# Residual product of an attention layer taken into the seven-product accumulation

## The chip, the cores and the metric

The kernel runs on one core of a Trainium2 chip. The metric is the device time in microseconds (us) of one execution. An engine runs its own instructions in the order in which the program gives them: PE (matrix products), DVE (vector), ACT (scalar functions), POOL and SP. SP and ACT also issue the DMA transfers here, in line with their other instructions.

## The reference, cut to what matters

Two layers work on x of shape (2, 512, 64, 64). Layer 0 (a deformable convolution) is not touched by the change. Layer 1 is attention over the 4096 pixels of each image, after a group normalization:

```
px = _gn(x) as (pixels, 512)
q, k = tanh(px @ Wq.T), tanh(px @ Wk.T)          # 64 features
scores = einsum('bip,bjp,p->bij', q, k, align_w)
content = px + softmax(scores) @ (px @ Wv.T)
content = content @ Wfc.T + bfc
out = relu(batch_norm(content)); x = x + out
```

The kernel takes Wfc into the values: content @ Wfc.T is px @ Wfc.T (the residual product) plus softmax(scores) @ (px @ (Wv.T @ Wfc.T)).

## The kernel before

Layer 1 handles one image after the other. First it projects keys and queries (`pk`, L1233) and values (`values`, L1196 to L1213: product `pv`, blocks stored to DRAM as `v_d`), in four rounds `i` of two pixel chunks each. Then it goes over eight query chunks `qb` of 512 pixels. For a chunk, the 4096 keys are taken as NPAIR = 16 pairs of two key blocks of 128.

`produce(qb, kp)` (L1167) makes the scores of a pair (`pS`), their exponentials `e` as four blocks (two key blocks by two halves of 256 queries), three combinations `tt` and one `t3` of these blocks, and adds the exponentials to `tots[qb]`. It runs two pairs ahead. A pair's product with its values, a 2 by 2 block product, is done with seven block products in place of eight (Strassen's scheme in Winograd's form): `v` holds seven combinations of value blocks, `operands` gives the moving side. Six of the products are summed over the pairs in six PSUM banks, `acc[0]` to `acc[5]` (L1271), each as two products of 256 columns. The other two banks, tag `st`, hold the scores. The seventh product is summed afterwards in bank 0, as `p7` (L1322), with `v7` (128 KB, six buffers, loaded by SP) and the sixteen `t3` that were kept.

Between the pairs and `p7` the banks are put together to `ct` (L1284 to L1291): ACT copies bank 0, DVE adds the others. The sum over keys comes from `pr` = ones x `tots` in bank 1 (L1293), `rin` is its reciprocal, and `ct` is multiplied by it (L1296). `residual(cb)` (L1305) makes the residual product for 128 output channels with four products of 512 columns (`pf`, banks 1 and 2), adds it and the bias to `ct`, and takes statistics for two of the four channel blocks. `residual(0)` stands ahead of `p7`, the three others are strewn into it. `produce` for the next chunk's first two pairs stands in `p7` too. `finish_chunk` then adds `p7`, scaled by `rin`, and takes the other statistics; it is advanced during the next chunk's pairs. The pixels `xq` of a chunk are loaded at pair 2 and normalized at pair 6; `xq` and `wc` (the weights of the values) share a tag with two buffers.

The order is written out by hand (`tc.manual_schedule()`), and every engine's order is the order of emission. In the last chunk of image 0, ACT issues six chunk loads for image 1 (`chunk`, L1126). In the last chunk of image 1, the pool of the key side is closed (`inner.close()`), eight tiles `res` (`xr`, 1 MB each) are taken from its space, and ACT issues their loads (L1303). After the last `p7`, the batch statistics are put together, and sixteen chunks are scaled, added to x and stored; image 0's chunks are fetched back for that (L1372, 2 MB each).

Of the kernel before, what the change touches and what calls it, by code (L numbers as in the profile page):

```python
# [570 lines left out]
def window_path(ctx: ExitStack, tc: tile.TileContext, t_in: dict, out: bass.AP, far: bass.AP, sums: bass.AP):  # L571
# [12 lines left out]
    def load(name, shape, src=None, pool=const):  # L584
        t = pool.tile(shape, F32, name=f"{name}_sb")
        nc.sync.dma_start(t, t_in[name] if src is None else src)
        return t

    def load_w(name, cols, pool):
        return load(name, [P, KB, cols], t_in[name].rearrange("(kb p) m -> p kb m", p=P), pool)  # L590
# [497 lines left out]
    with ExitStack() as l1, tc.manual_schedule():  # L1088
# [8 lines left out]
        with ExitStack() as at, ExitStack() as inner:  # L1097
# [31 lines left out]
            def value_output():  # L1129
                t = wk.tile([P, KB, C], F32, tag="x", name="wc")  # L1130
                nc.sync.dma_start(t, wc_d)
                return t
# [15 lines left out]
            wfc = load_w("wfcT", C, aw)  # L1148
# [45 lines left out]
            def operands(e, tt):  # L1194
                return (e[:, 0, :], e[:, 2, :], tt[:, 0, :], tt[:, 1, :], e[:, 3, :], tt[:, 2, :])

            def values(i, x1, x2, t):

                cols = slice(t * P, (t + 1) * P)
                pv = []  # L1200
                for h, x in enumerate((x1, x2)):
                    p = bank(2 * (t % 2) + h, "pv")
                    for kb in range(KB):
                        nc.tensor.matmul(p, x[:, kb, cols], wc[:, kb, :], start=(kb == 0), stop=(kb == KB - 1))  # L1204
                    pv.append(p)
                v = vw.tile([P, 7, HC], F32, name="v", bufs=4)
                nc.scalar.copy(v[:, 0, :], pv[0][:, :HC])
                nc.vector.tensor_sub(v[:, 6, :], v[:, 0, :], pv[0][:, HC:])
                nc.scalar.copy(v[:, 1:6:4, :], pv[1].rearrange("p (a c) -> p a c", a=2))
                nc.vector.tensor_add(v[:, 3, :], v[:, 5, :], pv[0][:, HC:])  # L1210
                nc.vector.tensor_sub(v[:, 2, :], v[:, 3, :], v[:, 0, :])
                nc.vector.tensor_sub(v[:, 4, :], v[:, 1, :], v[:, 2, :])
                nc.sync.dma_start(v_d[n][4 * i + t], v)  # L1213

# [10 lines left out]
            for n in range(NB):  # L1225
                sc, bi = norms[n]
                ready = []
                for i in range(NCH // 2):
                    for h in range(2):
                        ch = 2 * i + h  # L1230
                        pk = bank(4 + h, "pk")
                        for kb in range(KB):
                            nc.tensor.matmul(  # L1233
                                pk, wkq[:, h, kb].rearrange("p h d -> p (h d)"), xs[ch][:, kb, :],
                                start=(kb == 0), stop=(kb == KB - 1),
                            )
                        nc.scalar.activation(kq[:, ch, :], pk, AF.Tanh)
                    if i == 0:
                        queries(0)
                    for t in range(4):  # L1240
                        values(i, xs[2 * i], xs[2 * i + 1], t)
                        if t in (0, 1) and i + 1 < NCH // 2:
                            normalize(xs[2 * i + 2 + t], sc, bi)
                        if i + 1 == NCH // 2 and t in (1, 2):
                            produce(0, t - 1)
                        if i + 1 == NCH // 2 and t > 1:
                            ready.append(load_values(n, t - 2))
# [3 lines left out]
                for qb in range(NCH):  # L1251
                    acc = {}
                    for kp in range(NPAIR):
                        if kp + 2 < NPAIR:
                            produce(qb, kp + 2)
                        nxt = qb * NPAIR + kp + 2
                        if nxt < NCH * NPAIR:
                            ready.append(load_values(n, nxt % NPAIR))
                        if kp == 2:
                            xq = wk.tile([P, KB, CH], F32, tag="x", name="xq")  # L1260
                            nc.sync.dma_start(xq, x1_d[n][qb])
                        if kp >= NPAIR - 6:
                            v7s[kp - NPAIR + 6] = load_seventh(n, kp - NPAIR + 6)
                        v = ready.pop(0)
                        e, tt, _ = made[qb, kp]
                        ops = operands(e, tt)
                        for j in (3, 4, 5, 2, 1, 0) if kp == 0 else range(6):
                            if kp == 0:
                                acc[j] = bank(j, f"acc{j}")
                            for cb in range(2):  # L1270
                                nc.tensor.matmul(  # L1271
                                    acc[j][:, cb * HQ : (cb + 1) * HQ], v[:, j, cb * P : (cb + 1) * P], ops[j],
                                    start=(kp + cb == 0), stop=(kp + cb == NPAIR),
# [11 lines left out]
                    u = [wk.tile([P, 2, HQ], F32, name=f"u{j}", bufs=1) for j in range(2)]  # L1285
                    nc.scalar.copy(u[0], a[0])
                    nc.vector.tensor_add(ct[:, 0:2, 0:HQ], u[0], a[1])
                    nc.vector.tensor_add(u[1], u[0], a[2])
                    nc.vector.tensor_add(ct[:, 2:4, HQ:], u[1], a[3])
                    nc.vector.tensor_add(ct[:, 0:2, HQ:], ct[:, 2:4, HQ:], a[4])  # L1290
                    nc.vector.tensor_sub(ct[:, 2:4, 0:HQ], u[1], a[5])  # L1291
                    pr = bank(1, "pr")
                    nc.tensor.matmul(pr, ones, tots.pop(qb), start=True, stop=True)  # L1293
                    rin = wk.tile([P, CH], F32, name="rin", bufs=1)
                    nc.vector.reciprocal(rin, pr)
# [9 lines left out]
                    def residual(cb, ct=ct, xq=xq):  # L1305
                        pf = bank(1 + (cb + 1) % 2, "pf")
                        for kb in range(KB):
                            nc.tensor.matmul(  # L1308
                                pf, wfc[:, kb, cb * P : (cb + 1) * P], xq[:, kb, :], start=(kb == 0), stop=(kb == KB - 1)
                            )  # L1310
                        nc.vector.scalar_tensor_tensor(
                            ct[:, cb, :], pf, bfc[:, cb : cb + 1], ct[:, cb, :], ALU.add, ALU.add
                        )
                        if cb < 2:
                            nc.vector.bn_stats(bst[:, cb, n * NCH + qb, :], ct[:, cb, :])

                    residual(0)
                    p7 = bank(0, "p7")
                    for kp in range(NPAIR):
                        v7, t3 = v7s.pop(kp), made.pop((qb, kp))[2]  # L1320
                        for cb in range(2):
                            nc.tensor.matmul(  # L1322
                                p7[:, cb * HQ : (cb + 1) * HQ], v7[:, cb * P : (cb + 1) * P], t3,
                                start=(kp + cb == 0), stop=(kp + cb == NPAIR),
                            )
                        if kp + 6 < NPAIR:
                            v7s[kp + 6] = load_seventh(n, kp + 6)
                        if kp in (3, 7, 11):
                            residual(1 + kp // 4)
                        if qb + 1 < NCH and kp in (5, 9):  # L1330
                            produce(qb + 1, kp // 4 - 1)
                        if qb + 1 == NCH and n + 1 < NB:
                            if kp < 6:
                                xs[kp] = chunk(n + 1, kp)
# [5 lines left out]
                    def finish_chunk(qb=qb, ct=ct, p7=p7, rin=rin):  # L1340
                        t = wk.tile([P, 2, 2, HQ], F32, name="t7", bufs=1)
# [5 lines left out]
                        nc.vector.tensor_add(ct[:, 2:4, :], ct[:, 2:4, :], t.rearrange("p cb h q -> p cb (h q)"))  # L1347
# [98 lines left out]
```

## Time and profile before

| | us |
|---|---|
| median of 3 runs | 3756.47 (3755.73 to 3758.72) |
| profiled execution, its own time | 3756.61 |
| its span | 3754.8 |
| PE busy | 3472.1 |
| DVE busy | 2216.8 |
| ACT busy | 1270.2 |

Layer 1 begins at about 1280, its attention runs from about 1422 to 2478 (image 0) and from about 2616 to 3669 (image 1), and the end of the program follows. A line of a timeline has the start, the length, the engine, the source line, the operation and the tiles written and read; "x8" is a run of eight instructions, and brackets hold the idle time before and who ended it. PE instructions overlap at their ends, so the step from one start to the next is their price, not their listed length.

### The profile page before, as it was taken

The page shows a single profiled execution, that of the slowest core. Times are in us where ns is not written, and L with a number is a line of the kernel's source. Part 1 is how long each engine was busy: PE and PEld are TensorE (multiplying, and loading weights), DVE is VectorE, ACT ScalarE, POOL GpSimd, SP SyncE. Part 2 cuts the span into 40 slices and gives each one's busy share as a digit, 9 for nine tenths or more (in the row PEclk, how much of TensorE's full clock was granted, in tenths as well). Part 3 has the DMA queues.
Part 4 walks back from the last instruction along what each step waited for, and adds up shares of the span by engine and source line. Part 5 has one row for each costly group of instructions (what it writes and reads, how often), then busy time and mean ns, then how long its engine had stood idle before and what let it go on. Part 6 is the DMA issues. An engine that isn't in the chain of part 4 may idle for free.

```text
span 3754.8 us, 37118 instructions
## 1 busy us (share of the span) xinstructions
PE 3472.1 (92%) x14351; PEld 2287.0 (61%) x14351; DVE 2216.8 (59%) x3366; ACT 1270.2 (34%) x1624; POOL 221.4 (6%) x162
## 2 busy tenths in 40 slices
PE   4689989999998899999999999999999999999990
PEld 1255555555555446777777777754777777777770
DVE  5899989999996314444454444422454444445444
ACT  1466767777776322111111111122111111111114
POOL 2112112112111000000000000000000000000000
PEclk8789999999999899999999999999999999999995
DMA  6233432433423424334333433343433333333349
GB/s 236 62 97 124 135 122 81 130 115 100 132 83 107 174 99 174 130 117 140 126 125 123 138 131 116 132 175 135 144 120 119 110 137 114 111 132 120 119 163 381
DMA packets 179628, 499.94 MB, mean 133 GB/s; under 512 B 22096, under 2 KB 63824, under 8 KB 169968
## 3 DMA queue, kind: packets, MB, share of 16 engines
q1 hardware_dynamic: 176528, 476.48, 37.4%
q10 hardware_dynamic: 2880, 20.97, 1.4%
q8 instruction: 115, 1.88, 0.2%
q14 instruction: 73, 0.60, 0.0%
q0 software_dynamic: 32, 0.00, 0.0%
HBM read 406.09 MB, written 91.29 MB: 132 GB/s over the span
## 4 chain that ended last, share of the span: by engine, by line
PE 77%; DVE 15%; DMA 3%; ACT 2%; issue 1%; POOL 1%; SPq 1%; ACTq 0%; POOLq 0%; DVEq 0%
PE acc L1271 36%; DVE conv L786 9%; PE pS L1172 7%; PE pv L1204 6%; PE p L1322 6%; PE pf L1308 6%; PE pq L756 4%; PE py L967 4%; PE pa L947 4%; PE pk L1233 2%; PE p_mean L799 1%; DVE gn_st L711 1%; DMA v<-wv 1%; DVE pk L883 1%; DVE aw L888 1%
## 5 line engine op out<-in xcount | busy, mean ns | idle before, releaser
L1176 ACT ACTIVATE e<-pS 128x1024 f32<-128x1024 f32 x256 | 262.5, 1025 | 1557.4 <-PE pS L1172 1515.9
L1271 PE MATMUL acc<-e,v 128*128 128x256 f32 x3072 | 768.2, 386 | 1.7 <-DMA v<-wv 1.7
L1271 PE MATMUL acc<-tt,v 128*128 128x256 f32 x3072 | 748.3, 380 | 0.0
L1271 PEld LDWEIGHTS acc<-e,v 128*128 128x128 f32 x3072 | 566.5, 190 | 228.2 <-issue 156.2
L1271 PEld LDWEIGHTS acc<-tt,v 128*128 128x128 f32 x3072 | 582.4, 190 | 90.7 <-issue 10.6
L1179 DVE TENSOR_TENSOR t<-e 128x256 f32<-128x256 f32 x256 | 109.0, 426 | 742.4 <-ACT e L1176 742.4
L786 DVE SCALAR_TENSOR_TENSOR conv<-xn,L_conv_dw_w_sb,conv 128x504 f32<-128x504 f32 (+1 forms) x512 | 401.1, 797 | 20.8 <-DMA xt<-xj 5.3
L1189 DVE TENSOR_TENSOR tot<-tot,e 128x512 f32<-128x512 f32 x480 | 330.2, 688 | 8.3
L947 PEld LDWEIGHTS pa<-bt,patch 96*128 96x128 f32 x2048 | 251.7, 197 | 63.0 <-issue 38.9
L1172 PE MATMUL pS<-q,kq 64*128 64x512 f32 x1024 | 289.0, 641 | 0.0
L947 PE MATMUL pa<-bt,patch 96*128 96x128 f32 x2048 | 255.4, 281 | 9.2 <-ACT dT L958 5.8
L933 ACT COPY bt<-pb 96x1024 f32<-96x1024 f32 x124 | 233.8, 1998 | 58.9 <-PE pb L928 58.9
L967 PE MATMUL py<-dT,L_conv_out_w_sb 128*128 128x512 f32 x512 | 240.8, 616 | 0.0
L1322 PE MATMUL p<-t,v 128*128 128x256 f32 x1024 | 239.6, 382 | 1.2 <-DMA v<-wv 1.2
L756 PE MATMUL pq<-L_conv_in_w_sb,xn 128*128 128x512 f32 x512 | 237.2, 607 | 2.3 <-ACT xn L746 2.3
L1322 PEld LDWEIGHTS p<-t,v 128*128 128x128 f32 x1024 | 191.9, 190 | 75.8 <-issue 51.8
L1308 PE MATMUL pf<-xq,wfcT_sb 128*128 128x512 f32 x512 | 230.2, 592 | 0.0
L1204 PE MATMUL pv<-wc,xt 128*128 128x512 f32 x512 | 222.1, 593 | 0.0
L958 ACT COPY dT<-pa 32x256 f32<-32x256 f32 x496 | 180.3, 363 | 110.6 <-PE pa L947 101.3
L840 PE MATMUL po<-om_w_pg,feat 128*128 128x432 f32 x512 | 204.2, 543 | 0.0
L967 PEld LDWEIGHTS py<-dT,L_conv_out_w_sb 128*128 128x128 f32 x512 | 100.9, 201 | 122.0 <-issue 118.1
L1204 PEld LDWEIGHTS pv<-wc,xt 128*128 128x128 f32 x512 | 96.9, 190 | 123.6 <-issue 122.1
(158 smaller groups left out, 3062.0 us busy)
## 6 DMA issues: line engine op xcount, KB each, us to landing
v<-wv SPq DMA_DIRECT2D x256, 768.0 KB
patch<-xt SPq DMA_DIRECT2D x256, 192.0 KB
v<-wv SPq DMA_DIRECT2D x256, 128.0 KB
wv<-v SPq DMA_DIRECT2D x32, 896.0 KB
xt<-xj SPq DMA_DIRECT2D x128, 128.0 KB
res<-in_x SPq DMA_DIRECT2D x64, 256.0 KB
wx<-res SPq DMA_DIRECT2D x64, 256.0 KB
xq<-wx SPq DMA_DIRECT2D x16, 1024.0 KB
```

The costliest lines, as they stand in the source:

```text
L756: nc.tensor.matmul(pq, xn[:, kb, 1 + 2 * t : 3 + 2 * t, :].rearrange("p r c -> p (r c)"), in_w[:, kb, :], start=(kb == 0), stop=(kb == KB ...
L786: nc.vector.scalar_tensor_tensor(dst, src, wt, dst, ALU.mult, ALU.add)
L933: copy(bt[:SN].rearrange("s g q d -> s d (g q)")[:, d0 : d0 + 4, :], pb[:SN])
L947: nc.tensor.matmul(pa[:, p], xp[:SN, p, cb * P : (cb + 1) * P], bt[:SN, 4 * cb : 4 * cb + 4, PX * s + p, :], start=True, stop=True,)
L967: nc.tensor.matmul(py, out_w[:, kb, cb * P : (cb + 1) * P], dT[:, kb, :], start=(kb == 0), stop=(kb == KB - 1))
L1172: nc.tensor.matmul(pS[:, h, :], kq[r, 2 * (kp // 4) + h, c0 : c0 + P], qs[qb][r, :], start=True, stop=True)
L1176: nc.scalar.activation(e.rearrange("p a q -> p (a q)"), pS.rearrange("p h q -> p (h q)"), AF.Exp)
L1189: nc.vector.tensor_add(tots[qb], tots[qb], e2[:, h, :])
L1204: nc.tensor.matmul(p, x[:, kb, cols], wc[:, kb, :], start=(kb == 0), stop=(kb == KB - 1))
L1271: nc.tensor.matmul(acc[j][:, cb * HQ : (cb + 1) * HQ], v[:, j, cb * P : (cb + 1) * P], ops[j], start=(kp + cb == 0), stop=(kp + cb == NPAIR),)
L1308: nc.tensor.matmul(pf, wfc[:, kb, cb * P : (cb + 1) * P], xq[:, kb, :], start=(kb == 0), stop=(kb == KB - 1))
L1322: nc.tensor.matmul(p7[:, cb * HQ : (cb + 1) * HQ], v7[:, cb * P : (cb + 1) * P], t3, start=(kp + cb == 0), stop=(kp + cb == NPAIR),)
```

## The change

- `residual` is gone. The four channel blocks of the pixels count as two more pairs, 16 and 17, of "key blocks", and Wfc.T counts as their values. As `ct` is divided by the sum over keys at the end, the pixels are multiplied by that sum first: `xq` times `pr`, ahead of pair 15's products.
- `pr` moves from bank 1 to a score bank, ahead of pair 15; the combinations `tx` of the scaled pixels and `rin` are made there.
- `w7` holds the seven combinations of Wfc.T, made once (`output_weights`) in the third round of image 0, from a load that stood at the start of layer 1 and now takes a chunk buffer.
- The accumulation runs over 18 pairs, and so does `p7`; pair 16 takes the banks in the order 0, 1, 4, 2, 3, 5.
- The bias is added by ACT for two channel blocks and inside `finish_chunk` for the two others.
- In the last chunk of each image, the seventh values 6 to 15 are loaded into two buffers of `v` at pairs 14 and 15, in place of loads during `p7`.
- `xq` and `wc` have one buffer.

```diff
-                    for kp in range(NPAIR):
+                    for kp in range(NPAIR + 2):
...
+                        if kp == NPAIR - 1:
+
+                            pr = ps.tile([P, 2, CH], F32, tag="st", name="pr")[:, 0, :]
+                            nc.tensor.matmul(pr, ones, tots.pop(qb), start=True, stop=True)
+                            nc.vector.tensor_mul(xq, xq, pr.unsqueeze(1).to_broadcast([P, KB, CH]))
+                            x4 = xq.rearrange("p (h r) (j q) -> p h r j q", h=2, j=2)
+                            tx = wk.tile([P, 2, 4, HQ], F32, name="tx", bufs=1)
+                            nc.vector.tensor_sub(tx[:, :, 3, :], x4[:, 1, :, 1, :], x4[:, 0, :, 1, :])
+                            nc.vector.tensor_add(tx[:, :, 0, :], tx[:, :, 3, :], x4[:, 0, :, 0, :])
+                            nc.vector.tensor_sub(tx[:, :, 2, :], tx[:, :, 0, :], x4[:, 1, :, 0, :])
+                            nc.vector.tensor_sub(tx[:, :, 1, :], x4[:, 0, :, 1, :], x4[:, 0, :, 0, :])
+                            rin = wk.tile([P, CH], F32, name="rin", bufs=1)
+                            nc.vector.reciprocal(rin, pr)
...
+                        if qb + 1 == NCH and kp in (NPAIR - 2, NPAIR - 1):
+
+                            vg = vw.tile([P, 7, HC], F32, name="v", bufs=4)
+                            for m in range(7 if kp == NPAIR - 2 else 3):
+                                k7 = 6 + m + 7 * (kp - NPAIR + 2)
+                                nc.sync.dma_start(vg[:, m, :], v_d[n][k7][:, 6, :])
+                                v7s[k7] = vg[:, m, :]
+                        if kp < NPAIR:
+                            v = ready.pop(0)
+                            e, tt, _ = made[qb, kp]
+                            ops = operands(lambda k: e[:, k, :], tt)
+                        else:
+                            v = w7[:, kp - NPAIR]
+                            ops = operands(lambda k: x4[:, k // 2, kp - NPAIR, k % 2, :], tx[:, kp - NPAIR])
...
-                    pr = bank(1, "pr")
-                    nc.tensor.matmul(pr, ones, tots.pop(qb), start=True, stop=True)
-                    rin = wk.tile([P, CH], F32, name="rin", bufs=1)
-                    nc.vector.reciprocal(rin, pr)
...
-                    def residual(cb, ct=ct, xq=xq):
-                        pf = bank(1 + (cb + 1) % 2, "pf")
-                        for kb in range(KB):
-                            nc.tensor.matmul(
-                                pf, wfc[:, kb, cb * P : (cb + 1) * P], xq[:, kb, :], start=(kb == 0), stop=(kb == KB - 1)
-                            )
-                        nc.vector.scalar_tensor_tensor(
-                            ct[:, cb, :], pf, bfc[:, cb : cb + 1], ct[:, cb, :], ALU.add, ALU.add
-                        )
-                        if cb < 2:
-                            nc.vector.bn_stats(bst[:, cb, n * NCH + qb, :], ct[:, cb, :])
-
-                    residual(0)
...
-                    for kp in range(NPAIR):
-                        v7, t3 = v7s.pop(kp), made.pop((qb, kp))[2]
+                    for k in range(NPAIR + 2):
+                        kp = k - 2
+                        if kp < 0:
+                            v7, t3 = w7[:, k, 6, :], tx[:, k, 3, :]
+                        else:
+                            v7, t3 = v7s.pop(kp), made.pop((qb, kp))[2]
...
-                        if kp in (3, 7, 11):
-                            residual(1 + kp // 4)
+                        if kp in (6, 8):
+                            cb = kp // 2 - 3
+                            nc.scalar.activation(ct[:, cb, :], ct[:, cb, :], AF.Identity, bias=bfc[:, cb : cb + 1])
+                            nc.vector.bn_stats(bst[:, cb, n * NCH + qb, :], ct[:, cb, :])
...
-                        nc.vector.tensor_add(ct[:, 2:4, :], ct[:, 2:4, :], t.rearrange("p cb h q -> p cb (h q)"))
+                        for cb in (2, 3):
+                            nc.vector.scalar_tensor_tensor(
+                                ct[:, cb, :], t[:, cb - 2].rearrange("p h q -> p (h q)"), bfc[:, cb : cb + 1], ct[:, cb, :],
+                                ALU.add, ALU.add,
+                            )
...
+            def output_weights():
+
+                wfc = load_w("wfcT", C, cp, tag="c")
+                wf4 = wfc.rearrange("p (h r) (i c) -> p h r i c", h=2, i=2)
+                nc.scalar.copy(w7[:, :, 0, :], wf4[:, 0, :, 0, :])
+                nc.scalar.copy(w7[:, :, 1, :], wf4[:, 1, :, 0, :])
+                nc.scalar.copy(w7[:, :, 5, :], wf4[:, 1, :, 1, :])
+                nc.vector.tensor_sub(w7[:, :, 6, :], wf4[:, 0, :, 0, :], wf4[:, 0, :, 1, :])
+                nc.vector.tensor_add(w7[:, :, 3, :], wf4[:, 0, :, 1, :], wf4[:, 1, :, 1, :])
+                nc.vector.tensor_sub(w7[:, :, 2, :], w7[:, :, 3, :], w7[:, :, 0, :])
+                nc.vector.tensor_sub(w7[:, :, 4, :], w7[:, :, 1, :], w7[:, :, 2, :])
```

## The prediction

> **What bounds the kernel now.** I read the page first (shares, groups), then the timeline at the end of one query chunk, the busy time of short stretches, and the chain of waits at the end. The groups give the unit prices:
>
> ```profile
> L1271 PE MATMUL acc<-e,v 128*128 128x256 f32 x3072 | 768.2, 386 | 1.7 <-DMA v<-wv 1.7
> L1322 PE MATMUL p<-t,v 128*128 128x256 f32 x1024 | 239.6, 382 | 1.2 <-DMA v<-wv 1.2
> L1308 PE MATMUL pf<-xq,wfcT_sb 128*128 128x512 f32 x512 | 230.2, 592 | 0.0
> ```
>
> Each f32 product is two instructions: 16 chunks x 16 products of 512 columns are 512 records. PE lost under 3 us to waits in all three groups. The timeline where a chunk ends:
>
> ```profile
> 1788.00 0.59 ACT L1286 COPY u<-acc 128x512 f32<-128x512 f32 x1 [10.34 <-PE acc L1271]
> ...
> 1792.12 1.02 PE L1293 MATMUL pr<-tot,ones_k 128*128 128x512 f32 x2
> ...
> 1792.98 3.60 PE L1308 MATMUL pf<-xq,wfcT_sb 128*128 128x512 f32 x8
> ...
> 1793.18 3.36 DVE L1295 RECIPROCAL rin<-pr 128x512 f32<-128x512 f32 x1 [0.17 <-PE pr L1293]
> ...
> 1796.41 3.62 PE L1322 MATMUL p<-t,v 128*128 128x256 f32 x16
> 1796.41 3.21 PEld L1322 LDWEIGHTS p<-t,v 128*128 128x128 f32 x15 [0.24 <-issue]
> 1796.57 2.29 DVE L1296 TENSOR_TENSOR ct<-ct,rin 128x2048 f32<-128x2048 f32 x1
> ```
>
> Start to start, 8 `pf` instructions take 1796.41 - 1792.98 = 3.43 us, 0.429 each; 16 `p` instructions take 3.46 us (the next group starts at 1799.87), 0.216 each. No hole lies between the groups: attention is a solid stream of matmuls at full clock. The end is not:
>
> ```profile
> 3630.00:3640.00 10.00, 10.00 (x47) 8.59 (x46) 3.20 (x5) 0.59 (x1) 0.00 (x0) 1.00 0.00 0
> 3640.00:3645.00 5.00, 5.00 (x16) 2.72 (x15) 4.79 (x3) 0.00 (x0) 0.00 (x0) 1.00 0.81 333
> ...
> 3700.00:3710.00 10.00, 0.00 (x0) 0.00 (x0) 7.89 (x5) 10.00 (x15) 0.00 (x0) 0.50 1.02 423
> ...
> 3740.00:3750.00 10.00, 0.00 (x0) 0.00 (x0) 0.00 (x0) 0.00 (x0) 0.00 (x0) 0.50 1.05 408
> ```
>
> The columns are PE, PEld, DVE, ACT, POOL busy, clock, DMA share, GB/s. The DMA engines stand still until 3640 and are then full to the end. What starts them is ACT's queue:
>
> ```profile
> 3639.55 15.42 ACTq L1303 DMA_DIRECT2D xr<-wx  x8
> ```
>
> So 15 chunks are bound by PE, and the last one hands over to DMA: from 3641 to 3751 it moves 8.4 MB of `res`, 16.8 of fetches, 16.8 of outputs and 1.3 of seventh values (`v7`), 43.3 MB in 110 us, 393 GB/s.
>
> **The change part by part.**
>
> *Residual products.* Gone per chunk: 16 products of 512 columns, 32 instructions x 0.429 = 13.73 us. Added: two pairs of 12 products plus 4 for `p7`, each 256 columns, 28 products, 56 instructions x 0.216 = 12.09. Saved 1.64 us a chunk, 26.2 in 16. The added instructions have the shape and neighbours of L1271 and L1322. Bounds: 0.215 to 0.224 (24 products' instructions between two `pS`, 5.38 us / 24), so 1.2 to 1.7; I take 0.216, as no `pS` stands among most of them.
>
> Against this speaks the Trainium skill, "TensorE: Matmul & The Clock Gate", Part 3: a weight load overlaps running matmuls only when its row group differs. These loads are 128*128 and take 0.190. By that rule after costs 56 x (0.190 + 0.216) = 22.7 us and before 32 x (0.190 + 0.429) = 19.8: 2.9 slower a chunk, 47 in all. The row above has 15 loads inside 3.62 us of 16 matmuls, so here they do hide; the trace decides.
>
> *Sum and scaled pixels, moved ahead of pair 15.* `pr` (0.86 us of PE) only changes place. DVE then does the multiply (2.29, by L1296), four operations of 512 elements (0.69 by L1287, 2.75 together) and the reciprocal. In the last pairs before (3623 to 3639) the last sum is added by 3628.0 and PE reaches pair 15 at 3634.2, so `pr` waits for nobody. From the start of `pr`: sum at 1.06, multiply done 3.35, differences done 6.1; the reciprocal ends at 9.5. PE needs the first pixels at 0.86 + 5.18 = 6.04 and, with the order of pair 16, the differences from 8.6 on. Hidden by pair 15's products; without that cover it would cost some 2.5 us a chunk. `p7` needs bank 0, which is copied out after the first 4 of pair 17's 24 instructions, 4.3 us ahead: no wait. `pr` and `pf` needed banks 1 and 2 before, and waited for neither, so nothing is gained there. `xq` has one buffer now; its load at pair 2 waits for the last chunk's pair 17, long past, and `wc` finds it free when the image ends: zero.
>
> *Evictions.* DVE loses four `ct` additions (0.75) and one of 1024 (1.22) and gains 6.5 us with the two new ones: about +2.3 a chunk at 46% busy. ACT gains two of 0.80. Both sit in `p7`, where the next chunk's first two exponentials also lie; `p7` with its two `pS` lasts 17.7 us, DVE has about 10 us of work there (one addition, 2.29, two statistics of 0.69, 2.4 and 3.1 for the exponentials). Zero; uncovered it would be the sum of the new ones, 2.3 and 1.6 us a chunk.
>
> *Seventh values.* `p7` shrinks from 27.8 to 17.7 us, and ten loads of 128 KB must come in it, each let go five pairs (4.3 us) ahead. One issued at 1797.47 moves its bytes at 1798.5 to 1799.0, so about 1.7 us. Zero; see the rival.
>
> *Output weights.* The 1 MB load leaves the start, where PE did not wait for it (zero), and enters SP's queue behind the first value store of the third round, about 1372.8. With that store's 0.9 MB and at some 410 GB/s it lands near 1378.5. ACT stands in line behind it: three copies (1.8), `normalize` (2.9), then the copies that free banks 2 and 3, whose last reader ends about 6.2 us after landing, 1384.7; PE wants bank 2 at 1384.0. Between 0 and 2.7 us (2 us later landing); I take +0.7.
>
> *Image to image.* There a `v7` load held PE 0.67 us (the waits of that stretch: `p`, L1322, on `v<-wv`). Now all ten are loaded in pairs 14 and 15 into free `v` buffers, on SP ahead of `wc`, before the six chunk loads crowd the engines: -0.7. ACT's new bias steps queue behind the chunk loads, whose issue took 10.6 us; the first two chunks are normalized about 2 us before PE asks. Bounds -0.7 to +2; I take -0.7.
>
> *The tail.* The last chunk starts 15 x 1.64 + 0.7 - 0.7 = 24.6 us earlier. `res` no longer starts at the end of pair 15: on ACT it stands behind the copy of bank 0, which now ends with pair 17's first product: 0.86 + 28 x 0.216 + 0.8 = 7.7 after pair 15 against 0.2, so 7.5 later: net 17.1 earlier. Ten `v7` loads, 1.31 MB, are out of this stretch (they land while DMA is idle): 1.31 / 393 GB/s = 3.3 us. If DMA stays full, the end comes 20.4 us earlier. It should: five loads of `res` go out at once as before, the sixth when one lands, and the last two wait for `p7`'s end, as they lie over one of the two borrowed `v` buffers; that is 3.5 + 15.5 = 19 us after the first issue (rest of pair 17, then 72 instructions), and six loads and one fetch are 7.3 MB, 18 us. ACT's bias steps now come after these waits, so the statistics end about 3.3 us later after `p7` than before (two issues 0.75, two biases 1.6, a statistic 0.69, the split addition 0.28); with `p7`'s end 26.8 earlier the first output comes 23 us earlier; the loads fill DMA until then.
>
> Sum against the profiled execution (3756.61, span 3754.8): -20.4, 3736.2. The median of the runs shown is 3756.47, so **3736**.
>
> **The rivals.**
>
> *Everything is kept.* If the tail hangs on compute, not on bytes, the end moves with `p7`: 26.2 + 0.6 of `v7` stall, 27, less what the later statistics cost. 3730 to 3733. Against: DMA share 1.0 through the last 110 us. For: the stretch has dips (283 GB/s at 3652) that could vanish with the small loads.
>
> *DMA starves in the last chunk.* The held `res` loads leave the engines idle until `p7` ends, or the statistics hold outputs back after all loads are done: 3 to 8 us lost of the 20.4. 3739 to 3744. For: ACT issues in order and took 15.42 us over these 8. Against: the byte count above.
>
> *Slower: the seventh values don't keep up.* One mechanism, in `p7`, in 14 chunks. With six buffers a turnaround R over 4.3 us stalls PE about twice by R - 4.3. It eats the whole 20.4 at R = 5.0 (14 x 2 x 0.73). In the last chunk of before R was 8.3 (issued 3644.70, PE went on at 3652.99): then 8 us a chunk, 14 x 8 - 20 = 92 us slower, 3848. Against: that one shared the engines with five 1 MB loads; in ordinary chunks `p7` runs alone and R is about 2.
>
> That the residual products do not go away is ruled out by the diff.
>
> **How the numbers follow.** The likeliest 0.58 (3733 to 3739), everything kept 0.17, starving 0.18, the slower side 0.05, no change 0.02. A difference under 0.2%, 7.5 us, can't be told from none; all cases but the last two are beyond it. The range 3729 to 3744 takes in the first three.
>
> **What would show it.** The `pf` group gone; the `acc` groups with 6912 instructions in sum (6144 before), the `p7` groups with 1152 (1024); a multiply of about 2.29 us on `xq` during pair 15 and no PE wait behind it; each chunk's period shorter by 1.64 us; `res` first issued near 3622.5 and a DMA share of 1.0 from there to the end. PE waits on `v<-wv` in `p7` make the forecast too low by what they hold; holes in the DMA share after 3624 likewise; an end that moves with `p7` makes it too high.

## The result, and the profile after

| | before | after |
|---|---|---|
| median, us | 3756.1 (3755.57 to 3758.72) | 3729.63 (3727.62 to 3730.27) |
| ratio | | 0.9928, 95% interval 0.9916 to 0.9941 |
| profiled execution, its own time | 3756.61 | 3727.62 |
| its span | 3754.8 | 3725.8 |

The change makes the kernel 26.5 us faster; 20.4 were forecast. The new time lies at the lower end of the range given.

First the groups of after (the view that keeps shapes apart): line, engine, operation, tiles, count, busy us, mean ns, idle us before.

```profile
L1347 PE MATMUL p<-t,v 128*128 128x256 f32 x1024 | 231.1, 382 | 0.0
L1309 PE MATMUL acc<-xq,w 128*128 128x256 f32 x384 | 90.7, 379 | 0.0
L1309 PE MATMUL acc<-tx,w 128*128 128x256 f32 x384 | 90.7, 379 | 0.0
L1347 PE MATMUL p<-tx,w 128*128 128x256 f32 x128 | 30.2, 379 | 0.0
```

`pf` is gone, three groups have come, and every one of them, `p7` with the seventh values too, has 0.0 us of idle time before it. The same chunk's end as shown of before, in a timeline:

```profile
1780.82 1.02 PE L1273 MATMUL pr<-tot,ones_k 128*128 128x512 f32 x2
...
1781.68 1.89 PE L1309 MATMUL acc<-e,v 128*128 128x256 f32 x8
...
1781.88 2.29 DVE L1274 TENSOR_TENSOR xq<-xq,pr 128x2048 f32<-128x2048 f32 x1 [7.22 <-PE pr L1273]
...
1786.86 2.75 PE L1309 MATMUL acc<-xq,w 128*128 128x256 f32 x12
...
1789.45 2.75 PE L1309 MATMUL acc<-tx,w 128*128 128x256 f32 x12
```

The multiply ends at 1784.17, 2.7 us before PE reaches the scaled pixels. The step from one group of twelve to the next is 2.59 us, 0.216 an instruction. Then the final stretch, in windows of 5 us (columns as in the prediction; the second-last number is the DMA share, the last GB/s), and what ACT does there:

```profile
3615.00:3620.00 5.00, 5.00 (x25) 4.41 (x24) 1.08 (x3) 0.59 (x1) 0.00 (x0) 1.00 0.10 18
3620.00:3625.00 5.00, 5.00 (x25) 4.41 (x24) 4.44 (x5) 0.00 (x0) 0.00 (x0) 1.00 0.97 395
...
3645.00:3650.00 5.00, 0.37 (x1) 0.08 (x1) 2.57 (x10) 4.53 (x7) 0.03 (x1) 0.50 1.01 419
...
3715.00:3720.00 5.00, 0.00 (x0) 0.00 (x0) 0.00 (x0) 0.00 (x0) 0.00 (x0) 0.50 1.05 408
3720.00:3725.00 5.00, 0.00 (x0) 0.00 (x0) 0.00 (x0) 0.00 (x0) 0.00 (x0) 0.50 0.35 136
```

```profile
3618.45 17.91 ACTq L1337 DMA_DIRECT2D xr<-wx  x8
3636.41 1.33 ACT L1355 ACTIVATE ct<-ct,L_conv_bfc_sb 128x512 f32<-128x512 f32 x2 [17.61 <-PE p L1347]
...
3645.47 22.66 ACT L1421 ACTIVATE ct<-ct,bsh,bsc 128x512 f32<-128x512 f32 x32 [1.07 <-DVE bsh L1416]
```

DMA is full from about 3619.6 to 3722.5: 103 us for 42.0 MB, 408 GB/s. Before, the same stretch ran from about 3640.5 to 3751: 110.5 us for 43.4 MB, 393 GB/s.

To set executions side by side I take the first `gn_p` product of layer 1 (L602) as zero: it lies between 1273.4 and 1280.5 in the fourteen profiled executions told of here, in both kernels alike, and layer 0 is the same program in all of them. From there, in us:

| | attention starts | image 0's attention | values of image 1 | image 1 to last product's end | last product's end to the end | sum |
|---|---|---|---|---|---|---|
| before | 149.0 | 1049.6 | 141.0 | 1049.2 | 86.0 | 2474.9 |
| after | 150.7 | 1035.4 | 141.0 | 1035.6 | 87.7 | 2450.4 |
| difference | +1.7 | -14.2 | 0.0 | -13.6 | +1.7 | -24.5 |

So 24.5 us are layer 1's; the rest of the 26.5 is within the interval of the ratio and the scatter of layer 0.

### The profile page after: what moved, and what is told of

Same layout as the page of the kernel before. It is cut to its first block, busy times and chain, and to the rows that moved or that the text cites. A ratio compares the mean times of both kernels' runs of the same rounds, so it can differ in the third digit from the quotient of the medians.

```text
span 3725.8 us, 37930 instructions
## 1 busy us (share of the span) xinstructions
PE 3443.0 (92%) x14735; PEld 2359.8 (63%) x14735; DVE 2249.3 (60%) x3402; ACT 1290.7 (35%) x1659; POOL 220.5 (6%) x162
## 4 chain that ended last, share of the span: by engine, by line
PE 60%; DMA 1%; DVE 0%; ACT 0%; SPq 0%; issue 0%; ACTq 0%
PE acc L1309 41%; PE pS L1172 7%; PE p L1347 7%; PE pv L1204 4%; PE pk L1245 1%; DMA out<-ct 1%; PE pr L1273 0%; DMA v<-wv 0%; DMA r<-wx 0%; ACT ct L1421 0%; DVE r L1425 0%; SPq L1403 0%; ACT r L1421 0%; DVE ct L1425 0%; ACT e L1176 0%
## 5 line engine op out<-in xcount | busy, mean ns | idle before, releaser
L1347 PE MATMUL p<-t,v 128*128 128x256 f32 x1024 | 231.1, 382 | 0.0
L756 PEld LDWEIGHTS pq<-L_conv_in_w_sb,xn 128*128 128x128 f32 x512 | 94.5, 195 | 107.5 <-issue 94.1
```

The lines of the kernel that those rows point to most:

```text
L756: nc.tensor.matmul(pq, xn[:, kb, 1 + 2 * t : 3 + 2 * t, :].rearrange("p r c -> p (r c)"), in_w[:, kb, :], start=(kb == 0), stop=(kb == KB ...
L1347: nc.tensor.matmul(p7[:, cb * HQ : (cb + 1) * HQ], v7[:, cb * P : (cb + 1) * P], t3, start=(k + cb == 0), stop=(k + cb == NPAIR + 2),)
```

## The experiments

The table gathers what the experiments show of the final stretch, from the same zero. "First residual" is the first issue of a `res` load.

| run | median, us | first residual | last product's end | first output | end |
|---|---|---|---|---|---|
| before | 3756.1 | 2359.6 | 2388.9 | 2401.2 | 2474.9 |
| after | 3729.6 | 2343.0 | 2362.7 | 2375.3 | 2450.4 |
| e1 | 3729.2 | 2343.0 | 2362.6 | 2375.3 | 2450.6 |
| e2 | 3771.0 | 2388.1 | 2388.1 | 2414.7 | 2492.7 |
| e3 | 3749.4 | 2355.6 | 2386.0 | 2398.5 | 2471.9 |
| e4 | 3729.7 | 2336.8 | 2362.7 | 2375.4 | 2450.2 |
| e8 | 3760.3 | 2359.5 | 2387.9 | 2409.6 | 2482.5 |
| e9 | 3727.9 | 2341.4 | 2361.0 | 2370.5 | 2450.2 |
| e10 | 3729.0 | 2335.2 | 2361.1 | 2370.6 | 2451.9 |
| e11 | 3714.9 | 2343.5 | 2363.1 | 2375.8 | 2436.9 |
| e12 | 3744.2 | 2353.9 | 2362.7 | 2387.4 | 2465.0 |

**e1, the kernel after once more**, without an edit.

> The changed kernel once more, for a second profile. The change in the profiled executions was 29.0 us, of which 4.5 lie in layer 0, whose program is the same. Theory A (layer 0 differs from execution to execution): this profile starts layer 1 (first pk) anywhere from 1280 to 1286, and from there to the end it takes what the first profile of the changed kernel took, 2445.5 us, within 1. Theory B (the changed layout of layer 1 reaches back into layer 0): layer 1 starts within 1 us of 1280.3 again. Time about 27 us under before by both.

Measured: 3729.17 us (3727.18 to 3730.62), ratio 0.9926 (0.9913 to 0.994). Layer 1 took 2450.6 us against 2450.4, while its start moved by 2.5. In these two executions layer 1 repeats to a few tenths; what layer 0 gives or takes is not the change's.

**e5, the weight loads by themselves.** In the kernel before:

```diff
-                            nc.tensor.matmul(
-                                pf, wfc[:, kb, cb * P : (cb + 1) * P], xq[:, kb, :], start=(kb == 0), stop=(kb == KB - 1)
-                            )
+                            for h in range(2):
+                                nc.tensor.matmul(
+                                    pf[:, h * HQ : (h + 1) * HQ], wfc[:, kb, cb * P : (cb + 1) * P],
+                                    xq[:, kb, h * HQ : (h + 1) * HQ],
+                                    start=(kb + h == 0), stop=(kb + h == KB),
+                                )
```

> The kernel before, with each residual product of 512 columns cut into two of 256 (the same bytes and sums, 64 instructions a chunk for 32). It puts the dispute on weight loads by itself. Theory A (what the trace showed: the loads hide behind 256-column products, and time goes by columns): 64 x 0.216 = 13.82 us a chunk for 32 x 0.429 = 13.73, 0.1 x 16 = 1.5 us slower, about 3756. Theory B (a load overlaps matmuls only when its row group differs): 64 x (0.190 + 0.216) for 32 x (0.190 + 0.429), 6.2 us a chunk, 99 us slower, about 3853. If B held, the change's saving of 1.64 us a chunk would need another explanation.

Measured: 3755.45 us, ratio 1.0006 (0.9997 to 1.0015); layer 1 takes 2.3 us longer than before (2477.2). The timeline of e5:

```profile
1786.97 3.62 PE L1309 MATMUL pf<-xq,wfcT_sb 128*128 128x256 f32 x16
1790.42 3.62 PE L1325 MATMUL p<-t,v 128*128 128x256 f32 x16
```

Sixteen halves take 3.45 us from start to start, where eight whole ones took 3.43. From one chunk's `pr` to the next it is 131.47 us for 131.39, 0.08 more where 0.09 was expected. Twice the weight loads cost next to nothing. The rule of the Trainium skill that the prediction weighed ("TensorE: Matmul & The Clock Gate", Part 3) would have made this 99 us. So the saving is the one that was argued: fewer columns streamed, 28 x 256 in place of 16 x 512.

**e6, the cover taken from the scaling.** In after, the sum, the multiply and the differences are issued at pair 16:

```diff
-                        if kp == NPAIR - 1:
+                        if kp == NPAIR:
```

> After, with the sum product and the scaling of the pixels issued at pair 16 instead of ahead of pair 15, so that pair 15's products no longer cover them. Theory A (the cover is what makes them free): PE stands from the end of the sum product (0.86) to the end of the multiply (3.35), 2.5 us a chunk, and perhaps 0.2 more for the differences: 16 x 2.5 to 2.7 = 40 to 43 us slower than after, about 3771. Theory B (the additions to the sum and the seventh values leave slack elsewhere, or DVE does the multiply sooner): under 1 us a chunk, below 3746.

Measured: 3786.45 us (3782.74 to 3787.4), ratio 1.0087 (1.007 to 1.0104); layer 1 is 55.6 us longer than in after, more than Theory A gave. The waits of PE, and two windows behind one of them, the second a part of the first:

```profile
PE acc L1309 <- DVE xq L1274: 38.1, 16, 2.4
```

```profile
1665.00:1670.00 5.00, 4.62 (x15) 3.86 (x16) 4.90 (x6) 0.00 (x0) 0.00 (x0) 0.66 0.00 0
1666.00:1667.00 1.00, 1.00 (x4) 0.82 (x3) 0.93 (x3) 0.00 (x0) 0.00 (x0) 0.50 0.00 0
```

The wait itself is nearly as worked out: 16 of 2.4 us. A chunk that keeps its clock takes 132.39 us from `pr` to `pr`, where it takes 129.74 in after: 2.65 more, 42 in sixteen. The other 13 us are the clock: behind 8 of the 16 waits the granted clock (the column PEclk) is 0.50 for some 3.4 us, and such a chunk takes about 134.1, 1.7 more. So pair 15's products hide 3.5 us a chunk, not 2.5.

**e7, the turnaround of the seventh values.** In after, three buffers in place of six, and loads issued three pairs ahead:

```diff
-                v = wk.tile([P, HC], F32, name="v7", bufs=6)
+                v = wk.tile([P, HC], F32, name="v7", bufs=3)
...
-                        if 0 <= kp and kp + 6 < NPAIR and qb + 1 < NCH:
-                            v7s[kp + 6] = load_seventh(n, kp + 6)
+                        if 0 <= kp and kp + 3 < (NPAIR if qb + 1 < NCH else 6):
+                            v7s[kp + 3] = load_seventh(n, kp + 3)
```

> After, with three buffers for the seventh values instead of six; each load is let go two pairs (8 products, 1.73 us) before it is wanted instead of five (4.3 us). It measures the turnaround R that the rival of the slower side hangs on. With R = 1.7 nothing is lost: 3730. With R = 2.0 each round of three loads takes 0.86 + 2.0 = 2.86 us for 2.59, 0.27 x 13/3 x 14 chunks = 16 us: 3746. With R = 3.0, 77 us: 3807. With R near 5, the value at which the rival would have eaten the gain, some 200 us: 3930.

Measured: 3778.95 us (3773.6 to 3784.91), ratio 1.007 (1.0054 to 1.0087); layer 1 is 50.5 us longer. The timeline of an ordinary chunk's `p7`:

```profile
1803.69 2.75 PE L1347 MATMUL p<-t,v 128*128 128x256 f32 x12
1806.87 2.86 PE L1347 MATMUL p<-t,v 128*128 128x256 f32 x12 [0.43 <-DMA v<-wv]
```

Twelve instructions are 2.59 us, and the next three pairs start after 3.18; with 0.86 for the pair that frees a buffer, R is 2.3 us. An ordinary chunk loses 2.2 us (its `p7` with its scores takes some 21.4 us for 19.2), 30 in fourteen. Nearly all the rest, some 20 us, falls in the two last chunks of the images, where loads of 1 MB are in flight and the first wait is 5.9 us. So six buffers, with 4.3 us of lead, have 2 us to spare in ordinary chunks, and little against 1 MB loads.

**e3, after without the early seventh values** in the last chunk of an image (they are loaded during `p7`, as in other chunks):

```diff
-                        if qb + 1 == NCH and kp in (NPAIR - 2, NPAIR - 1):
-
-                            vg = vw.tile([P, 7, HC], F32, name="v", bufs=4)
...
-                        if 0 <= kp and kp + 6 < NPAIR and qb + 1 < NCH:
+                        if 0 <= kp and kp + 6 < NPAIR:
```

> The changed kernel without that part: in the last chunks the seventh values are loaded during p7, which now lasts 15.5 us and not 29. Theory A: PE waits for them in both p7 (turnaround about 8 us beside 1 MB loads against 4.3 of lead, two rounds: some 8 us each), and the final DMA stretch grows by 7: time 12 to 16 us over the changed kernel. Rival (bytes only, and the turnaround stays near 2): 3 to 4 us.

Measured: 3749.41 us (3745.5 to 3753.96), ratio 0.9986 (0.998 to 0.9993); 21.5 us of layer 1. Its group of `p7`:

```profile
L1340 PE MATMUL p<-t,v 128*128 128x256 f32 x1024 | 240.4, 391 | 13.9 <-DMA v<-wv 13.9
```

Six waits sum to 13.9 us, and the clock falls behind them here too (to 0.69 and 0.50 in two of the windows after). Before, the residual products stood between the seventh products and gave these loads their time; without them the early loading is needed. It is worth 20 us to after; in the kernel before, the next two runs show no gain from it.

**e2 and e8, the early seventh values alone,** put into the kernel before (the lines removed in e3, added there). e2 reads the values 13 to 15 first in that `p7`. e8 keeps the order and issues the `res` loads in another:

```diff
-                            nc.scalar.dma_start(res[ch], x1_d[n][ch])
+                        for ch in (1, 2, 3, 4, 5, 6, 7, 0):
+                            nc.scalar.dma_start(res[ch], x1_d[n][ch])
```

> The kernel before with one part of the change: in the last chunk of each image seventh values 6 to 15 come in two v buffers at pairs 14 and 15, not in p7 (p7 takes pairs 13 to 15 first there, so that their buffer comes free early). Residual products as before. Theory A (these ten small loads cost the final DMA stretch far more than their bytes: 7 us): the stretch from the first res load to the end falls from 115.2 to about 108, and with the two stalls of 0.6 gone the time falls by 7 to 8. Rival (they cost their bytes at the mean rate, 3.3 us; the rest of the gain at the end came from elsewhere): 3.5 to 4.5 us.

> The kernel before, with only the seventh values of each image's last chunk loaded early into two free value buffers, as after has it; the residual input whose tile lies over such a buffer is issued last, so that it holds up no other. What of the gain comes from this part alone, and what did the small loads cost in the final stretch? Theory A (they cost their bytes): 1.31 MB at 393 GB/s = 3.3, and 0.7 us of the wait between images: 4.0 us faster, about 3751. Theory B (with rows of 1 KB among the 1 MB loads they cost more than bytes, as the dips to 174 to 283 GB/s suggest): the final stretch runs at 408 GB/s throughout, 42.0 MB in 103 us instead of 110: 7 to 8 faster, about 3748. Theory C (the end is set by the statistics and outputs behind the last product): the last product ends about 1.2 us earlier and the end with it: 2 faster, 3753.

Measured: e2 3771.03 us (3765.87 to 3771.95), ratio 1.0036 (1.0022 to 1.005); e8 3760.34 us (3755.73 to 3764.32), ratio 1.0019 (1.0011 to 1.0026). Both are slower, and no theory had that. ACT's queue in e2, then in e8:

```profile
3664.57 18.61 ACTq L1310 DMA_DIRECT2D xr<-wx  x8
```

```profile
3635.08 37.61 ACTq L1311 DMA_DIRECT2D xr<-wx  x8
3672.72 1.28 ACT L1388 ACT_TABLE_LOAD   x1 [41.37 <-DMA r<-wc]
```

By the program's addresses the first residual tile lies, in e2, over the borrowed buffer that is read last; so all eight loads stand until the last product's end. In e8 that buffer lies under the tiles of the last two loads: six are issued by 3643.3, the seventh at 3660.9, and DMA stands still from 3652 to 3661 (share 0.01). The eighth, at 3672.4, waited for the landing of a fetch that SP had issued at 3661.31, as the profile has it. ACT's table load and square root stand behind these issues, so the first output comes 8 us late, and the end with it. The last product itself came 1.0 us earlier in e8 (1.2 were forecast); the price of the small loads is not measured by either run.

**e4, an earlier start of the residual loads.** In after:

```diff
-                            nc.scalar.dma_start(res[ch], x1_d[n][ch])
+                            (nc.sync if ch < 6 else nc.scalar).dma_start(res[ch], x1_d[n][ch])
```

> The changed kernel with the first six res loads issued by SP, not by ACT behind the copy of bank 0: they start at the end of pair 15, 7 us earlier; the last two and the fetches as before. Theory A (the end hangs on bytes from the first res load on): the end comes about 4 to 6 us earlier, 7 less a gap of 1 to 3 us before pair 12 of p7 gives the next buffers free. Rival (the end hangs on the statistics and the outputs behind p7): within 1 us of the changed kernel.

Measured: 3729.7 us (3727.53 to 3732.62), ratio 0.9932 (0.9918 to 0.9946), the same as after. The loads did start 6.2 us earlier. Windows of e4:

```profile
3630.00:3635.00 5.00, 5.00 (x25) 4.41 (x24) 0.00 (x0) 0.00 (x0) 0.00 (x0) 1.00 0.22 90
...
3650.00:3655.00 5.00, 0.00 (x0) 0.00 (x0) 3.95 (x3) 5.00 (x8) 0.00 (x0) 0.50 1.00 371
...
3665.00:3670.00 5.00, 0.00 (x0) 0.00 (x0) 4.08 (x2) 5.00 (x8) 0.00 (x0) 0.50 0.94 325
```

The lead is used up by 3630: the next loads need tiles that the last product still holds, and DMA idles for about 5 us. What is left of it goes in two dips. So an earlier start alone does not move the end.

**e9 and e10, earlier statistics.** In the last chunk `p7` is made in two halves of 128 output channels, the second in bank 1, so that the first half's statistics lie beside it; the last two `res` loads are issued behind the biases; and the combinations of the output weights are issued three value steps behind their load. e10 also puts the first six `res` loads on SP.

```diff
+                        if n == 0 and i == 2 and t == 0:
+                            wfc = load_w("wfcT", C, cp, tag="c")
-                        if n == 0 and i == 2 and t == 0:
+                        if n == 0 and i == 2 and t == 3:
                             output_weights()
...
+                        if end:
+                            sevenths.append((v7, t3))
+                            nc.tensor.matmul(p7[:, :HQ], v7[:, :P], t3, start=(k == 0), stop=(k == NPAIR + 1))
...
+                        for k, (v7, t3) in enumerate(sevenths):
+                            nc.tensor.matmul(p7b[:, :HQ], v7[:, P:], t3, start=(k == 0), stop=(k == NPAIR + 1))
+                        finish_half(2, p7)
```

> After with two edits. The output weights' copies and differences are issued three value steps behind their load (the load stays where it is), so that ACT doesn't stand behind it: the wait of 1.4 us in the value rounds should go, and 1.7 us with it. In the very last chunk the seventh product is made in two halves, the first 128 output channels for all 18 pairs and then the others, so that the statistics of the first half lie beside the second; and ACT's two biases stand ahead of the last two residual loads. What follows the last product shrinks by about 3.2 us (1.21 + 1.41 + 1.28 + 1.91 = 5.81 of DVE to 2.6). Theory A (behind the last product the end hangs on bytes, 34.4 MB at full DMA share): only the first edit counts, 1.7 us faster than after, about 3728; the first output starts 3 us earlier and the end does not follow. Theory B (the end hangs on the statistics and outputs): 1.7 + 3.2, about 3724.5.

> The same, with the first six residual loads on SP's queue too, so that they start about 6 us earlier, as in the earlier run that gave nothing by it. Theory A (bytes left behind the last product): those loads bring about 0.6 MB more ahead of the last product, and the outputs, 3 us earlier, free the buffers whose lack cost that run its lead in two dips: 1.5 to 2.4 us over the run with the split alone, about 3726. Theory B (the outputs alone): the same as the split alone, about 3724.5.

Measured: e9 3727.91 us (3727.4 to 3732.38), ratio 0.9929 (0.9915 to 0.9942); e10 3728.99 us (3722.9 to 3732.23), ratio 0.9926 (0.9912 to 0.994). Neither can be told from after, so no version here beats it. The wait for the output weights is gone (attention starts at 149.0 again), and the first output comes 4.8 us earlier. The end does not: 2450.2 and 2451.9. In e9 that is Theory A's reading of the split, but the 1.7 us at the start did not arrive at the end either. e10 missed both numbers; it started loads and outputs earlier together, and DMA idled between them (share 0.46 to 0.77 from 3625 to 3640).

**e11, fewer bytes.** After without the eight fetches of image 0's residual input; each of its rows is added to itself in their place, so the output leaves that input out:

```diff
-            for k, src in enumerate((c0_d, x1_d[0])):
+            for k, src in enumerate((c0_d,)):
...
-                ct, xr = (last[ch], res[ch]) if n + 1 == NB else ready[ch]
+                ct, xr = (last[ch], res[ch]) if n + 1 == NB else (ready[ch] + ready[ch])
```

> After, leaving out the eight loads of the first image's residual input in the final stretch (its rows are added to themselves instead, so that part of the output is left wrong; all other work stays): 8.4 MB fewer of the 34.4 MB that DMA still has to move when the last product ends. Theory A (behind the last product the end hangs on bytes): 8.4 MB / 408 GB/s = 20.6 us faster than after, about 3709. Theory B (ACT's 64 rectifications of 0.71 us each, 22.66 / 32, and the outputs behind them set the end): the first output comes no sooner and the stretch shrinks by a few us at most, 3724 to 3729.

Measured: 3714.88 us (3714.66 to 3719.18), ratio 0.9894 (0.9877 to 0.991), 13.5 us off layer 1, between the two theories. Windows of e11:

```profile
3650.00:3655.00 5.00, 0.37 (x1) 0.08 (x1) 2.57 (x13) 3.98 (x6) 0.50 (x2) 0.50 0.63 256
3655.00:3660.00 5.00, 0.00 (x0) 0.00 (x0) 3.94 (x3) 5.00 (x8) 0.00 (x0) 0.50 0.56 204
...
```

The next two have 369 and 286 GB/s. Against 408 these four windows lack 2.6 MB, 6.3 us; 20.6 less 6.3 is 14.3. With a fifth of the bytes gone, DMA runs out of work before the first output. In after there is just enough to load until then: 1.9 MB of loads are left at its first output.

**e12, the small loads put back** into the last chunk of after, read by nobody:

```diff
+                        if 0 <= kp and kp + 6 < NPAIR and qb + 1 == NCH and n + 1 == NB:
+                            load_seventh(n, kp + 6)
```

> After, with ten loads of 128 KB of seventh values put back into the last chunk's product, into buffers that nobody reads then; the product itself still reads the early ones. It prices the small loads in the final stretch, as the prediction did at 1.31 MB / 393 GB/s = 3.3 us. Theory A (bytes): 3.2 to 3.3 us slower than after, about 3733. Theory B (rows of 1 KB cost DMA as much as the dips of the kernel before suggest, and they are why its stretch ran at 393 instead of 408): 6 to 7 us slower, about 3736.5. Theory C (they fall where DMA waits for buffers anyway): under 1 us.

Measured: 3744.2 us (3740.28 to 3745.89), ratio 0.9971 (0.9961 to 0.9981), 14.6 us slower in layer 1: no theory had that. The queues of SP and ACT:

```profile
3626.41 5.37 SPq L1234 DMA_DIRECT2D v<-wv  x10
```

```profile
3630.53 13.21 ACTq L1337 DMA_DIRECT2D xr<-wx  x8
3643.78 1.33 ACT L1357 ACTIVATE ct<-ct,L_conv_bfc_sb 128x512 f32<-128x512 f32 x2 [23.69 <-DMA v<-wv]
```

The residual loads did not start until the small ones were on their way, 10.9 us later than in after, and the biases and the first output followed, 12 us late. The program's own waits say why: all transfers of SP and ACT use eight completion semaphores in turn, each waits until the transfer eight places ahead of it has landed, and here the small loads have the places ahead of the residual ones. In the trace the third and the eighth residual load are issued 0.02 us after a small load has landed. So e12 does not price the bytes; 10.9 us of delay and 3.2 for 1.31 MB at 408 GB/s would make 14.1. It shows something else: the last product ended where it did in after (2362.7), and the end still came 14.6 us later. The end does not simply follow the last product.

## Why the prediction was right, and where it missed

The forecast was 3736, and the mechanism that it named is the one found. The measured time lies below the likeliest part (3733 to 3739) and only 0.6 us inside the whole range, which takes in two rivals as well: the forecast was right in kind and too small. In layer 1 the forecast gave 20.4 us and 24.5 were measured; the missing 4.1 come of one step, the tail's small loads.

- *Residual products.* Forecast 1.64 us a chunk; from `pr` to `pr` it is 129.74 us for 131.39, 1.65. Image 0's attention shrank by 14.2: eight chunks at 1.65 are 13.2, the wait between the images 0.7, and 0.3 is left over. The price of 0.216 held, and e5 shows by itself that twice the weight loads cost next to nothing.
- *Sum and scaled pixels.* Hidden as forecast. e6 shows what stands behind the zero: the wait of 2.5 us was about right (2.65 lost), but uncovered it costs 3.5, as the clock falls after half of the waits.
- *Evictions.* Zero: the `p7` groups have no idle time before them.
- *Seventh values.* Zero, with R at 2.3 us (e7) against a lead of 4.3; the forecast took R about 2. It gave `p7` 17.7 us; with its scores it takes 19.2 (27.8 before), a wrong sum that changed nothing. The slower rival would have needed R = 5.0 in ordinary chunks.
- *Output weights.* Forecast +0.7, bounds 0 to 2.7; measured +1.7:

```profile
1375.38 0.62 ACT L1219 COPY w<-wfcT_sb 128x512 f32<-128x512 f32 x1 [8.77 <-DMA wfcT_sb<-in_wfcT]
...
1381.12 7.13 PE L1204 MATMUL pv<-wc,xt 128*128 128x512 f32 x16 [1.40 <-DVE v L1210]
```

  The load was issued at 1368.46 and took 6.9 us; ACT stood 8.8 us in line behind it, its normalization followed, and the copies for PE came 1.4 us late. Layer 1 began 4.5 us earlier here than in the execution of before, so the forecast landing at 1378.5 reads 1374.0 on this clock: it came 1.4 us later than worked out. e9 takes the wait away.
- *Image to image.* The 0.7 is there: no `v7` wait is left.
- *The tail, start.* `res` was forecast to start net 17.1 us earlier. From the common zero its first load was issued at 2343.0 after 2359.6: 16.6. The prediction had five loads going out at once "as before"; before issued four, and the fifth 11.9 us later, and after issued six.
- *The tail, small loads: the step that was too small.* The prediction gave the missing 1.31 MB their bytes at the old mean rate, 3.3 us, and so kept 393 GB/s for what remained. From the first residual load to the end it was 115.3 us before and is 107.4 in after, 7.9 less; 16.6 and 7.9 are the 24.5 measured. Of the 7.9 the bytes at 408 GB/s are 3.2. The rest are dips that before had. Its queues of SP and ACT, a wait of SP, and windows:

```profile
3644.70 0.32 SPq L1222 DMA_DIRECT2D v<-wv  x1
...
3652.97 2.00 ACTq L1303 DMA_DIRECT2D xr<-wx  x4
```

```profile
SPq L1372 <- PE pf L1308: 4.8, 1, 4.8
```

```profile
3652.00:3653.00 1.00, 0.43 (x3) 0.03 (x2) 0.21 (x1) 0.00 (x0) 0.00 (x0) 1.00 0.86 283
3653.00:3654.00 1.00, 1.00 (x5) 0.90 (x6) 0.00 (x0) 0.00 (x0) 0.00 (x0) 1.00 0.77 198
...
3666.00:3667.00 1.00, 1.00 (x6) 0.81 (x5) 0.09 (x1) 0.00 (x0) 0.00 (x0) 1.00 0.89 174
...
3685.00:3690.00 5.00, 0.00 (x0) 0.00 (x0) 4.03 (x2) 5.00 (x9) 0.00 (x0) 0.50 1.01 370
```

  The first dip (285 GB/s from 3650 to 3655) is 1.5 us against 410. The first four residual loads had run out at 3652, and ACT issued the fifth at 3652.97, 0.02 us after the small load of 3644.70 had landed: it has the semaphore of that load (see e12). Until then only small rows moved. Beside loads of 1 MB they cost no more than their bytes: 410 and 424 GB/s from 3655 to 3665. The second dip (335 from 3665 to 3670) is 0.9 us: SP's first fetch waited 4.8 us for the last residual product and was issued at 3665.33, when the residual loads were running out; in after it was issued at 3624.25. The third, 2.5 us, lies in four windows from 3680 on (364, 370, 348 and 350): at the first output 0.4 MB of the loads were left, where after has 1.9, and then outputs of 1.05 MB come one in 2.8 us, 372 GB/s. Together with the bytes this makes 8.1 for the 7.9. So the small loads cost more than their bytes because they held up a large one, and two of the dips had another cause. All this is read from the waits and windows of the two traces. No run took the dips away one by one: e2, e8 and e12 were made to price the small loads, and each moved the residual loads instead.
- *The tail, statistics.* Forecast 3.3 us later behind the last product, measured 0.4 (7.44 us from its end to the first rectification, 7.07 before). The last two residual loads were issued at 3635.5, when `p7` had read seventh value 12, not at its end: by the program's addresses the first borrowed buffer lies under them, not the second. So the biases started 1.6 us before the end of `p7`.
- *The rivals.* "Everything is kept" came nearest with its number, 3730 to 3733, but not with its reason. It took compute to set the end; outputs 4.8 us earlier (e9) did not move it, and 8.4 MB fewer (e11) did. What it said of the dips, that they could vanish, is what happened. Starving was not seen in after, only where loads were held back (before, e2, e4, e8, e10) or taken out (e11).

What sets the end of after is thus no single thing. When the last product ends, 34.5 of the 42.0 MB are still to move, 84.6 us at 408 GB/s, and DMA is full. It can't move more before (the tiles are held, e4), a later start with more bytes costs both (e12: 14.6 us for 10.9 and 1.31 MB), and fewer bytes gain until the first output limits them (e11). By these numbers the bounds lie within a few us of each other.

## What to carry to other kernels

Price a DMA stretch by its full-rate windows and list its dips separately; its mean rate hides what can go away. For each dip, ask which load should have been issued and what it waited for. A change that takes work out from between small loads takes their cover too, so look for the loads that the removed work was hiding (e3: 20 us). When tiles are taken from a pool that is being closed, what lies under each tile decides when its load starts, and on an in-order queue one held load holds all behind it. A small load can hold up a large one of another queue if the two share a completion semaphore.

## What the runs showed of the hardware

- A wait of PE of 2.4 us was enough to lower the granted clock to 0.50 for some 3.4 us behind 8 of 16 such waits (e6). The Trainium skill ("TensorE: Matmul & The Clock Gate", Part 1) gives an idle window of about 3.4 us for that; half of the waits here did it with less.
- Loads of 128 KB in rows of 1 KB, beside loads of 1 MB in rows of 8 KB, left the rate as it was: 410 and 424 GB/s in the two windows of before from 3655 to 3665. Alone they moved at 283 GB/s, with a DMA share of 0.86 (3652 to 3653).
- SP issued six such loads one behind the other, waiting for nobody, from 3594.87 to 3597.24 of after: 0.47 us each.
- The same program reached layer 1 between 1273.4 and 1280.5 us in fourteen executions; from there on two executions of after differ by 0.2 us.
